# Two-layer recurrent and attention block: one weight prepared from splits throughout, two lower parts built by adding DMAs, and a new order of down products, norm and mixer

## The chip, the cores and the metric

The kernel runs on one core of one Trainium2 chip. The metric is the device time of one execution in microseconds, the median of several runs. The engines are named as the profile names them: PE (TensorE, matrix products; PEld is its weight load), DVE (VectorE), ACT (ScalarE), POOL (GpSimd) and SP (SyncE, which here only issues DMAs). Each engine runs its own instructions in the order that was fixed when the kernel was built, and waits for others through semaphores.

## What is computed

The input x has 4 sequences (the batches b = 0 to 3 below) of 512 rows with 256 columns. There are two layers, and each does `x = x + s * g`, with `xn = layernorm(x)`, a mixer s and a gate g:

```python
# layer 0
s = xn + rmsnorm(y(xn) @ W_out.T, norm_w)   # y is linear in xn: one 256x256 matrix after preparation
g = silu(ffn(xn, W1, W2, W3))
# layer 1
s = attention(layernorm(xn)) + xn           # causal, one head of 256
g = silu(ffn(xn, W1, W2, W3))

def ffn(x, W1, W2, W3):
    hidden = silu(x @ W1.T) * (x @ W3.T)    # 1024 wide
    return fwht(hidden) @ W2.T              # fwht: Hadamard transform of the 1024 columns
```

The recurrence of layer 0 starts from a zero state and is taken for a single step, so it is linear in xn. The Hadamard transform is linear too, so the kernel applies it to W2 once, and never to the hidden values.

## The kernel before

**Splits.** Products must be nearly as exact as fp32. `split` (L59) makes two parts of a tile: `hi`, a copy by ACT rounded to a reduced format (F32R), and `lo = src - hi`, a subtraction by DVE. A product of two split operands is three products: hi·hi, hi·lo and lo·hi (`mm3`, L80; the order is all hi·hi first, then hi·lo and lo·hi in turn for each piece of the contraction). Products of F32R operands are the cheap kind on PE; a product of plain fp32 operands is one instruction in the program and a pair of records in the profile.

**Stages.** Layer 0 is a loop over batches (L997). For each batch `ffn` (L461) goes through 8 chunks of 128 hidden columns: two up products of `mm3` into PSUM banks (`gu`, three banks in turn; chunk 1 of batch 0 borrows two others), SiLU by ACT (L522), the gate multiply by DVE (L523), the split of the result (`hh`, `hl`), and then the down products of an earlier chunk. `defer` says how many chunks wait in the queue before the oldest is taken: all eight in batch 0 (`defer` is NH, since w2 isn't ready), one in batches 1 to 3. In batch 0 the upper parts of the first four chunks go to spare tiles (`early`), and their lower parts are made late, two each in chunks 6 and 7.

**Work beside.** After each half chunk `ffn` calls `slot`, and the object `Beside` (L876) then steps through a list of generators: each task has a number of steps, and slot k of 16 runs steps until the share done is (k + 1)/16 of the total number; the last slot runs all that is left. In batch 0 the tasks are, in this order:

- `prep_first` (L957, 12 steps). It runs `prep_w2` for layer 0: three butterfly steps on DVE for each of two column halves of w2 (scratch tiles come from the pool of the x tiles), then a Hadamard product of 128 on PE. For the first half of layer 0 (`native`, L156) that product takes the fp32 tile and the fp32 matrix `had_f` as they are; for the others the tile is split first and two products with `had` follow (L168). In between come `load_x(1)`, the load of the next batch on SP, and `prep_m` (L187), which builds the mixer's matrix m from win and wout: a scaled split of wout (`wg`), a split of win (`wi`), and 24 products (`mps`).
- `mixer(0)` (L709, 3 steps): products of the transposed xn with m (`o`), squares on ACT, a power on POOL, scaling and adding on DVE. What it adds to xn is used by the gate of batch 0 (`gate_all`), the first task of batch 1.
- `norm(0, 1)` (L426, 3 steps): layer norm of the next batch, its transposes on PE (`xt_1tp`), and their split (`xt`).

In slots of batch 0 the work is queued behind the gate multiply on DVE and behind the last up product on PE (L542).

**w13.** The weights W1 and W3 come in four quarters (q = 0 to 3), each loaded to `w13raw` and split by `split_w13` (L118) when its first chunk (2q) is reached in the program; quarter 0 in two halves.

**Layer 1.** From the end of batch 3 the order on PE is written out by hand (`line["fixed"]`, L66 and L1069): `ffn_s` (L556) has 8 places in each of four rounds q, and the lists in L1085 to L1117 say which steps of attention go there. `pv` (L853) multiplies the softmax by the values and, for each second tile, updates xn by DVE (L871). In round 1, place 7 holds `pv[0]` and `pv[1]`, just after the gate multiply of that round (L668).

Tiles of 4 KB a partition come from one pool of ten (`t4`), which w13raw, w2raw, win, wout and all splits of the preparation share; a tile is taken when an earlier one is free.

Of the kernel before, what the change touches and what calls it, by code (L numbers as in the profile page):

```python
# [11 lines left out]
F32 = mybir.dt.float32  # L12
# [9 lines left out]
P = 128  # L22
# [13 lines left out]
def kernel(ctx: ExitStack, tc: tile.TileContext, a: dict, out: bass.AP):  # L36
# [22 lines left out]
    def split(src, hi, lo, engine=nc.vector):  # L59

        h = nc.scalar.copy(hi, src)  # L61
        return h, engine.tensor_tensor(lo, src, hi.bitcast(F32), ALU.subtract)  # L62

    line = {"fixed": False, "last": None}  # L66
# [10 lines left out]
    def transpose(*args):  # L77
        return in_line(nc.tensor.transpose, *args)

    def mm3(o, terms):  # L80

        seq = [(l[0], r[0]) for l, r in terms]
        for l, r in terms:
            seq += [(l[0], r[1]), (l[1], r[0])]
        for n, (l, r) in enumerate(seq):
            ins = matmul(o, l, r, start=n == 0, stop=n == len(seq) - 1)
        return ins
# [30 lines left out]
    def split_w13(layer, q, raw):  # L118
        both = wp.tile([P, 2, 2, S], F32R, tag="w13", name=f"w13_{layer}_{q}", bufs=4)
        hi, lo = both[:, 0], both[:, 1]  # L120
        if (layer, q) != (0, 0):
            split(raw, hi, lo)
            return hi, lo
        halves = [slice(c * D, (c + 1) * D) for c in range(2)]
        split(*(z[:, :, halves[0]] for z in (raw, hi, lo)))
        next(normed)
        with after(first["norm"][0]), after(first["norm"][1]):
            hi_, lo_ = split(*(z[:, :, halves[1]] for z in (raw, hi, lo)))
        first["w13"] = hi_, lo_
        return hi, lo  # L130
# [8 lines left out]
    def prep_w2(layer, raws, dst, scratch):  # L139

        w2h, w2l = dst
        for half in range(2):
            ds_ = slice(half * P, (half + 1) * P)
            cur = raws[half]
            for st, h in enumerate((1, 2, 4)):
                nxt = scratch(f"w2b{st}_{layer}_{half}", [P, NH, P])
                cv = cur.rearrange("p (g two h) d -> p g two (h d)", two=2, h=h)
                nv = nxt.rearrange("p (g two h) d -> p g two (h d)", two=2, h=h)  # L150
                nc.vector.tensor_tensor(nv[:, :, 0], cv[:, :, 0], cv[:, :, 1], ALU.add)
                nc.vector.tensor_tensor(nv[:, :, 1], cv[:, :, 0], cv[:, :, 1], ALU.subtract)
                cur = nxt
                yield

            native = layer == 0 and half == 0  # L156
            if not native:
                bh = t4(f"w2bh_{layer}_{half}", [P, NH, P], F32R)
                bl = t4(f"w2bl_{layer}_{half}", [P, NH, P], F32R)
                split(cur, bh, bl)  # L160
                yield
            for q in range(2):
                o = psum(f"w2ps_{layer}_{half}_{q}", [P, NH // 2, P])
                qs = slice(q * NH // 2, (q + 1) * NH // 2)
                if native:
                    matmul(o, had_f, cur[:, qs, :], start=True, stop=True)
                else:
                    matmul(o, had, bh[:, qs, :], start=True, stop=False)  # L168
                    matmul(o, had, bl[:, qs, :], start=False, stop=True)
                split(o, w2h[:, qs, ds_], w2l[:, qs, ds_])  # L170
                yield

# [11 lines left out]
        nc.sync.dma_start(win, a["w_in"].rearrange("(c p) i -> p c i", p=P))  # L184
        return win, wout

    def prep_m(win, wout):  # L187

        cb = wp.tile([P, 4, 2, DS], F32, name="cb")
        nc.vector.tensor_tensor(cb, bc[:, :, 0:2, :], bc[:, :, 2:4, :], ALU.mult)  # L190
        cbd = wp.tile([P, 4, DS], F32, name="cbd")
        nc.vector.tensor_tensor(cbd, cb[:, :, 0, :], cb[:, :, 1, :], ALU.subtract)
        g = wp.tile([P, 4], F32, name="g")
        nc.vector.tensor_reduce(g, cbd, AX.X, ALU.add)
        wg = [t4(f"wg{i}", [P, 4, D], F32R) for i in "hl"]
        wi = [t4(f"wi{i}", [P, 4, D], F32R) for i in "hl"]
        for c in range(4):
            nc.scalar.mul(wg[0][:, c, :], wout[:, c, :], g[:, c : c + 1])
            nc.vector.scalar_tensor_tensor(
                wg[1][:, c, :], wout[:, c, :], g[:, c : c + 1], wg[0][:, c, :].bitcast(F32),  # L200
                ALU.mult, ALU.subtract,
            )
        split(win, *wi)
        yield
        hi, lo = (wp.tile([P, 2, D], F32R, name=f"m{i}") for i in "hl")
        o = psum("mps", [P, 2, D])
        for i in range(2):
            mm3(
                o[:, i, :],
                [(tuple(z[:, k, sl(i)] for z in wi), tuple(z[:, k, :] for z in wg)) for k in range(4)],  # L210
            )
        split(o, hi, lo)
        first["m"] = hi, lo
        yield
# [246 lines left out]
    def ffn(name, xT, w13, w2, slot, defer=1, spare=(), parts=1, behind=False, tail=()):  # L461
# [34 lines left out]
        for c in range(NH):  # L496
# [8 lines left out]
            for half in range(parts if c == 0 else 1):  # L505
                n = S // (parts if c == 0 else 1)
                ts_ = slice(half * n, (half + 1) * n)
                if parts == 1 or c:
                    for o, cols in gu:
                        last_up = mm3(o[:, ts_], k_pairs((wh, wl), cols, xT, ts_))  # L510
                    continue

                for n, (w, x) in enumerate(((wh, xT[0]), (wl, xT[0]), (wh, xT[1]))):
                    for o, cols in gu:
                        for k in range(2):
                            last_up = matmul(
                                o[:, ts_], w[:, k, cols], x[:, k, ts_],
                                start=n + k == 0, stop=n + k == 3,
                            )
# [189 lines left out]
    def mixer(b):  # L709

        xn, xT, m = xns[0, b], xTs[0, b], first["m"]
        osb = t4(f"osb{b}", [P, NT, D])
        r = small(f"ssr{b}")
        junk = t2(f"junk{b}", [P, D])
        for i in range(2):
            o = psum(f"o0_{b}_{i}", [P, 2, D])
            for j in range(2):
                mm3(o[:, j, :], k_pairs(xT, sl(2 * i + j), m, ALLD))
            nc.scalar.copy(osb[:, 2 * i : 2 * i + 2, :], o)
            for t in (2 * i, 2 * i + 1):  # L720
                nc.scalar.activation(junk, osb[:, t, :], AF.Square, accum_out=r[:, t : t + 1])
            yield
        nc.vector.tensor_scalar(r, r, 1.0 / D, RMS_EPS, ALU.mult, ALU.add)
        nc.gpsimd.tensor_tensor(r, r, mhalf, ALU.pow)
        for t in range(NT):
            nc.vector.scalar_tensor_tensor(
                osb[:, t, :], osb[:, t, :], r[:, t : t + 1], nwb, ALU.mult, ALU.mult
            )
        nc.vector.tensor_tensor(xn, xn, osb, ALU.add)
        yield  # L730

    class Attention:
# [45 lines left out]
        def tq(self, j):  # L778
            b = self.b
            if j == 0:  # L780
                self.tqs = t4(f"tqh{b}", [P, 2, S], F32R), t4(f"tql{b}", [P, 2, S], F32R)
            o = psum(f"tq{b}_{j}", [P, S])
            mm3(o, k_pairs(first["wqk"], sl(j), self.xg, ALLS))
            split(o, self.tqs[0][:, j, :], self.tqs[1][:, j, :])

        def v(self, i, j):
# [66 lines left out]
        def pv(self, i):  # L853
# [13 lines left out]
                ],  # L867
            )
            if i % 2:
                for t in (i - 1, i):  # L870
                    nc.vector.scalar_tensor_tensor(  # L871
                        xn[:, t, :], self.o[:, t % 2, :], self.rden[:, t : t + 1], xn[:, t, :],
                        ALU.mult, ALU.add,
                    )

    class Beside:  # L876

# [79 lines left out]
    def prep_first():  # L957
# [1 line left out]
        with after(first["w13"][1]):  # L959
            next(steps)  # L960
        yield
        for _ in range(4):
            next(steps)
            yield
        with after(first["silu"]):
            nc.scalar.copy(had, had_f)
        for _ in range(2):
            next(steps)
            yield
        for _ in range(2):  # L970
            next(steps)
            yield
        load_x(1)
        product = prep_m(*raw_m)
        next(product)
        yield
        next(steps)
# [19 lines left out]
    for b in range(B):  # L997
        tasks = []
        if b == 0:
            prep = prep_first()  # L1000
            next(prep)
            tasks.append((prep, 12))
        if b:
            tasks.append((call(gate_all, f"g0_{b - 1}", dn, xns[0, b - 1], xs[b - 1]), 1))
        tasks.append((mixer(b), MIXER))
        if b + 1 < B:
            if b:
                load_x(b + 1)
            if b == 2:
                tasks.append((prep_s(0), 4))  # L1010
            tasks.append((norm(0, b + 1), NORM))
        if b == 0:
            early = w2_tile("early0"), w2_tile("early1")
            spare = [
# [18 lines left out]
        if b == 0:  # L1033
            dn = ffn("f0_0", xTs[0, 0], w13, w2, bg.slot, NH, spare, parts=2, behind=True)
        else:
            tail = [run(atts[0].tq, j) for j in range(2)] if b + 1 == B else []
            dn = ffn(f"f0_{b}", xTs[0, b], w13, w2, bg.slot, tail=tail)
        bg.finish()


# [146 lines left out]
```

## Time and profile before

| | |
|---|---|
| median of 3 runs | 360.51 us (360.42 to 360.60) |
| the profiled execution | 360.78 us |
| its span in the profile | 359.0 us, 6278 instructions |
| DMA | 52.25 MB, mean 146 GB/s |

The profiler records one execution. Its span runs from the first to the last recorded instruction; the 1.8 us between span and time lie around it. In rows of the timeline the columns are the start in us, the time in us, the engine, the line of the source, the operation, the tiles written and read, the shape, and in brackets the idle time before it and what ended it. "f_0gu" is the up product of batch 0, "f_0dn" its down product; in layer 1 the same prefix is used with a round and a letter behind it ("f_0gu2z": batch 0, round 2, bank z). Many lines of the source are helpers (L70 is every matrix product, L61 and L62 are every split), so rows are told apart by their tiles.

The first 36 us, in four stretches of 9 us. The columns are the stretch, its length, busy time and number of instructions of PE, PEld, DVE, ACT and POOL, the granted clock of PE, the DMA share and the rate:

```profile
0.00:9.00 9.00, 7.55 (x28) 6.14 (x29) 5.44 (x17) 3.26 (x6) 1.80 (x7) 1.00 0.70 236
9.00:18.00 9.00, 9.00 (x50) 7.68 (x49) 8.00 (x13) 6.39 (x11) 0.00 (x0) 1.00 0.95 339
18.00:27.00 9.00, 9.00 (x36) 6.59 (x36) 9.00 (x17) 5.77 (x11) 0.00 (x0) 1.00 0.31 93
27.00:36.00 9.00, 9.00 (x51) 7.77 (x50) 9.00 (x17) 5.80 (x11) 0.00 (x0) 1.00 0.58 202
```

PE's ends are modelled, so a 9.00 there says only that no large gap was seen. The starts of successive products tell more.

### The profile page before, as it was taken

To read this page: it belongs to the slowest core of one execution; us is meant where nothing else is said; L and a number is where in the kernel's file an instruction comes from. 1 tells how busy PE (TensorE), PEld (TensorE's weight loads), DVE (VectorE), ACT (ScalarE), POOL (GpSimd) and SP (SyncE) were. 2 spreads that over 40 slices of the span, in tenths; PEclk is the share of its full clock that TensorE was granted. 3 is DMA by queue.
4 is the path that set the end of the run, shared out by engine and by line. 5 is a ranking of instruction groups with operands and counts; after the bars stand their busy time and mean duration, and the time that the engine had idled before them with its cause. 6 is when DMAs were issued, how large, how long until landed. Compare 5 with 4: busy or idle time off the path is not lost.

```text
span 359.0 us, 6278 instructions
## 1 busy us (share of the span) xinstructions
PE 352.4 (98%) x2477; PEld 328.1 (91%) x2477; DVE 287.5 (80%) x597; ACT 197.8 (55%) x373; POOL 20.8 (6%) x22
## 2 busy tenths in 40 slices
PE   8999999999999999999999999999999999999995
PEld 6878998888988898888999999999999999999995
DVE  6899648998579938998886957989669997567645
ACT  3766156266463425674467655576555676556443
POOL 2000110300020210100110001100011000000000
PEclk9999999999999999999999999999999999999999
DMA  7925000301044316656256045572554655445501
GB/s 235 341 91 206 2 1 2 99 18 60 0 157 165 150 39 233 248 180 195 105 207 263 16 190 206 203 224 103 204 179 165 207 186 204 136 151 192 197 2 58
DMA packets 16285, 52.25 MB, mean 146 GB/s; under 512 B 1633, under 2 KB 7937, under 8 KB 16257
## 3 DMA queue, kind: packets, MB, share of 16 engines
q1 hardware_dynamic: 15968, 51.60, 40.9%
q8 instruction: 19, 0.31, 0.4%
q10 hardware_dynamic: 288, 0.26, 0.2%
q14 instruction: 10, 0.07, 0.1%
HBM read 42.40 MB, written 9.45 MB: 144 GB/s over the span
## 4 chain that ended last, share of the span: by engine, by line
PE 96%; DVE 2%; ACT 1%; issue 0%; DVEq 0%
PE f_1dn L70 6%; PE f_2dn L70 6%; PE f_1gu L70 6%; PE f_0gu L70 6%; PE f_2gu L70 6%; PE f_3gu L70 6%; PE f_3dn L70 6%; PE f_0dn L70 6%; PE sc L70 4%; PE pv L70 4%; PE o L70 3%; PE v L70 3%; PE tq L70 3%; PE warm L70 2%; PE w2ps L70 1%; PE pt L70 1%
## 5 line engine op out<-in xcount | busy, mean ns | idle before, releaser
L70 PE MATMUL f_1gu<-xt,w 128*128 128x512 f32 x96 | 24.9, 397 | 0.3 <-ACT xt L61 0.3
L70 PE MATMUL f_3gu<-xt,w 128*128 128x512 f32 x96 | 25.0, 396 | 0.0
L70 PE MATMUL f_2gu<-xt,w 128*128 128x512 f32 x96 | 24.8, 395 | 0.0
L70 PE MATMUL f_0gu<-xt,w 128*128 128x512 f32 (+1 forms) x108 | 24.3, 378 | 0.0
L70 PEld LDWEIGHTS f_0gu<-xt,w 128*128 128x128 f32 x108 | 18.4, 188 | 4.4 <-issue 1.0
L70 PEld LDWEIGHTS f_1gu<-xt,w 128*128 128x128 f32 x96 | 17.0, 188 | 3.6 <-ACT xt L61 0.5
L70 PEld LDWEIGHTS f_2gu<-xt,w 128*128 128x128 f32 x96 | 17.0, 188 | 3.0
L70 PEld LDWEIGHTS f_3gu<-xt,w 128*128 128x128 f32 x96 | 17.0, 188 | 2.9
L61 ACT CAST f_2hh<-f_2h 128x512 fp32r<-128x512 f32 x16 | 9.9, 622 | 15.4 <-DVE f_2h L523 12.3
L70 PE MATMUL f_3dn<-w2l,f_3hh 128*128 128x256 f32 x64 | 17.7, 281 | 0.0
L70 PE MATMUL f_3dn<-w2h,f_3hh 128*128 128x256 f32 x64 | 17.7, 281 | 0.0
L70 PE MATMUL f_1dn<-w2l,f_1hh 128*128 128x256 f32 x64 | 17.7, 282 | 0.0
L70 PE MATMUL f_2dn<-w2h,f_2hh 128*128 128x256 f32 x64 | 17.7, 282 | 0.0
L70 PE MATMUL f_1dn<-w2h,f_1hh 128*128 128x256 f32 x64 | 17.7, 281 | 0.0
L70 PE MATMUL f_2dn<-w2l,f_2hh 128*128 128x256 f32 x64 | 17.6, 281 | 0.0
L70 PE MATMUL f_3dn<-w2h,f_3hl 128*128 128x256 f32 x64 | 17.0, 282 | 0.0
L70 PE MATMUL f_1dn<-w2h,f_1hl 128*128 128x256 f32 x64 | 17.0, 281 | 0.0
L70 PE MATMUL f_2dn<-w2h,f_2hl 128*128 128x256 f32 x64 | 16.7, 281 | 0.0
L61 ACT CAST f_3hh<-f_3h 128x512 fp32r<-128x512 f32 (+1 forms) x17 | 10.0, 594 | 10.2 <-DVE f_3h L523 6.1
L61 ACT CAST f_1hh<-f_1h 128x512 fp32r<-128x512 f32 x16 | 9.9, 622 | 9.7 <-DVE f_1h L523 6.6
L62 DVE TENSOR_TENSOR f_2hl<-f_2h,f_2hh 128x512 fp32r<-128x512 f32 x16 | 10.9, 682 | 3.9 <-ACT f_2hh L61 3.8
L70 PE MATMUL f_0dn<-w2l,f_0hh 128*128 128x256 f32 x48 | 13.7, 286 | 0.0
(487 smaller groups left out, 1147.6 us busy)
## 6 DMA issues: line engine op xcount, KB each, us to landing
sw<-s SPq DMA_DIRECT2D x32, 896.0 KB, 6.4
s<-sp SPq DMA_DIRECT2D x8, 512.0 KB, 3.8
s<-sp SPq DMA_DIRECT2D x8, 384.0 KB, 2.8
w2raw<-in_w SPq DMA_DIRECT2D x4, 512.0 KB, 5.6
sraw<-in_w SPq DMA_DIRECT2D x4, 512.0 KB, 4.3
mrb<-there SPq DMA_DIRECT2D x4, 512.0 KB, 3.7
w13raw<-in_w SPq DMA_DIRECT2D x3, 512.0 KB, 7.1
x<-in_x SPq DMA_DIRECT2D x3, 512.0 KB, 3.6
```

What stands on the lines that cost most here:

```text
L61: h = nc.scalar.copy(hi, src)
L62: return h, engine.tensor_tensor(lo, src, hi.bitcast(F32), ALU.subtract)
L70: ins = call(*args, **kwargs)
```

## The change

1. **w2 of layer 0.** `native` goes: both halves are split and multiplied by `had`. `prep_first` has 13 steps instead of 12, and the cast of `had` comes one step earlier.
2. **Two lower parts by DMA.** A new helper, `split_by_dma`: ACT writes the negated source to `lo`, then the rounded copy to `hi`, and a DMA issued by POOL adds the source to `lo`. It is used for quarter 3 of w13, and for win, whose split moves from `prep_m` into `prep_first`, before the second half of w2.
3. **Order in a sum of three products.** `mm3` takes `late`, which says whose lower part is used last: with 1 the right operand's (the default 0: the left's).
4. **Tasks of batch 0.** `norm(0, 1)` comes ahead of `mixer(0)`, and its steps aren't counted in the total, which is 16 instead of 18.
5. **Down products.** `defer` is 2 instead of 1 in batches 1 to 3.
6. **Attention.** The update of xn in `pv` is queued on DVE behind the last gate multiply (`first["gate"]`).

```diff
+    def split_by_dma(src, hi, lo):
+        nc.scalar.mul(lo, src, -1.0)
+        nc.scalar.copy(hi, src)
+        nc.gpsimd.dma_start(lo.bitcast(F32), src, accum_op=ALU.add)
...
-    def mm3(o, terms):
+    def mm3(o, terms, late=0):
         seq = [(l[0], r[0]) for l, r in terms]
-        for l, r in terms:
-            seq += [(l[0], r[1]), (l[1], r[0])]
+        for side in (1 - late, late):
+            seq += [(l[1 - side], r[side]) for l, r in terms]
...
-        if (layer, q) != (0, 0):
-            split(raw, hi, lo)
+        if q:
+            (split_by_dma if q == 3 else split)(raw, hi, lo)
             return hi, lo
...
-            native = layer == 0 and half == 0
-            if not native:
-                bh = t4(f"w2bh_{layer}_{half}", [P, NH, P], F32R)
-                bl = t4(f"w2bl_{layer}_{half}", [P, NH, P], F32R)
-                split(cur, bh, bl)
-                yield
+            bh, bl = (t4(f"w2b{i}_{layer}_{half}", [P, NH, P], F32R) for i in "hl")
+            split(cur, bh, bl)
+            yield
...
-                if native:
-                    matmul(o, had_f, cur[:, qs, :], start=True, stop=True)
-                else:
-                    matmul(o, had, bh[:, qs, :], start=True, stop=False)
-                    matmul(o, had, bl[:, qs, :], start=False, stop=True)
+                matmul(o, had, bh[:, qs, :], start=True, stop=False)
+                matmul(o, had, bl[:, qs, :], start=False, stop=True)
...
-    def prep_m(win, wout):
+    def prep_m(wi, wout):
...
-        wi = [t4(f"wi{i}", [P, 4, D], F32R) for i in "hl"]
...
-        split(win, *wi)
...
-                        last_up = mm3(o[:, ts_], k_pairs((wh, wl), cols, xT, ts_))
+                        last_up = mm3(o[:, ts_], k_pairs((wh, wl), cols, xT, ts_), late=int(not behind))
...
-                mm3(o[:, j, :], k_pairs(xT, sl(2 * i + j), m, ALLD))
+                mm3(o[:, j, :], k_pairs(xT, sl(2 * i + j), m, ALLD), late=1)
...
-            mm3(o, k_pairs(first["wqk"], sl(j), self.xg, ALLS))
+            mm3(o, k_pairs(first["wqk"], sl(j), self.xg, ALLS), late=1)
...
-                for t in (i - 1, i):
-                    nc.vector.scalar_tensor_tensor(
+                with after(first["gate"]):
+                    for t in (i - 1, i):
+                        nc.vector.scalar_tensor_tensor(
...
-        for _ in range(4):
+        for _ in range(3):
             next(steps)
             yield
         with after(first["silu"]):
@@
-        for _ in range(2):
+        win, wout = raw_m
+        wi = [t4(f"wi{i}", [P, 4, D], F32R) for i in "hl"]
+        split_by_dma(win, *wi)
+        for _ in range(4):
             next(steps)
             yield
         load_x(1)
-        product = prep_m(*raw_m)
+        product = prep_m(wi, wout)
...
-            tasks.append((prep, 12))
+            tasks.append((prep, 13))
...
-        tasks.append((mixer(b), MIXER))
+        if b:
+            tasks.append((mixer(b), MIXER))
...
-            tasks.append((norm(0, b + 1), NORM))
+            tasks.append((norm(0, b + 1), NORM if b else 0))
+        if b == 0:
+            tasks.append((mixer(b), MIXER))
...
-            dn = ffn(f"f0_{b}", xTs[0, b], w13, w2, bg.slot, tail=tail)
+            dn = ffn(f"f0_{b}", xTs[0, b], w13, w2, bg.slot, 2, tail=tail)
```

More of the change, by code (lines that the diff above doesn't have):

```diff
@@ L869, in pv @@
             if i % 2:
-                for t in (i - 1, i):
[L871 to L874, printed above, removed]
+                with after(first["gate"]):
+                    for t in (i - 1, i):
+                        nc.vector.scalar_tensor_tensor(
+                            xn[:, t, :], self.o[:, t % 2, :], self.rden[:, t : t + 1], xn[:, t, :],
+                            ALU.mult, ALU.add,
+                        )
     class Beside:
```

## The prediction

> **What bounds the kernel now.** I read the shares of busy time first, then the chain that ended last.
>
> ```profile
> PE 352.4 (98%) x2477; PEld 328.1 (91%) x2477; DVE 287.5 (80%) x597; ACT 197.8 (55%) x373; POOL 20.8 (6%) x22
> PE 96%; DVE 2%; ACT 1%; issue 0%; DVEq 0%
> ```
>
> PE is 96% of the chain: from its first real product at 8.16 us to the last gate at 354.9 us nearly every microsecond is a product. So I price every edit by one question: does PE do less, or wait less? VectorE or ScalarE time that is saved or added counts only where it makes PE wait. The granted clock is 1.00 in every stretch I asked for, so products cost the same everywhere: starts of successive 128x512 products are 0.233 us apart (6 in 1.40 us in the chain), of 128x256 products 0.118 us.
>
> To find PE's waits I went along the starts of its products, looking for a distance above these. Leaving the start-up, four places stand out. Two are work of an expensive kind, in the chain in order of time:
>
> ```profile
> 18.22 0.86 PE w2ps L70 x2
> 19.07 1.40 PE f_0gu L70 x6
> 20.48 0.86 PE w2ps L70 x2
> ```
>
> Each pair of records is one product of the plain fp32 Hadamard matrix with half of w2's first column half (L166), 0.86 us; the same shape from split operands costs 0.233 us a product. The other two are true waits. Layer 0, from batch 0 to batch 1 (timeline of PE):
>
> ```profile
> 51.18 0.28 PE L70 MATMUL f_0dn<-w2h,f_0hl 128*128 128x256 f32 x1
> 51.79 0.73 PE L70 MATMUL f_1gu<-xt,w 128*128 128x512 f32 x2 [0.33 <-ACT xt L61]
> ```
>
> The starts lie 0.61 us apart where 0.12 would do: 0.49 us, waiting for ScalarE's cast of batch 1's transposed input. And layer 1, batch 0 (timeline of all engines):
>
> ```profile
> 193.61 0.87 DVE L871 SCALAR_TENSOR_TENSOR xn<-pv,rden,xn 128x256 f32<-128x256 f32 x2
> ...
> 194.03 0.60 PE L70 MATMUL xt_1tp<-ident,xn 128*128 128x128 f32 x4
> ...
> 194.40 0.68 DVE L668 TENSOR_TENSOR f_0h<-f_0h,f_0gu1l 128x512 f32<-128x512 f32 x1
> ...
> 195.22 0.94 PE L70 MATMUL f_0gu2z<-tb,sw 128*128 128x256 f32 x6 [0.59 <-DVE f_0h L668]
> ```
>
> The four transposes would be through at 194.03 + 4 x 0.11 = 194.47; the next product starts at 195.22: 0.75 us lost. It needs the PSUM bank that L668 reads, and VectorE did two residual updates (L871) first.
>
> **Part by part.** *w2 from splits.* Removed: two native products, 2 x 0.86 = 1.72 us of PE. Added: four split products, 4 x 0.233 = 0.93. **-0.78 us**, with nothing beside it to hide it. Also added: one ScalarE cast (row w2bh, 1.05 us) and one VectorE subtraction (row w2bl, 1.21 us). They make half 0's w2 later, but its first use is by a down product at 32.49, and the last butterfly of that half ended at 16.73 + 0.68 = 17.41; plus 2.3 us is 19.7. Covered.
>
> *Norm ahead of the mixer.* Batch 1's normalised input was complete at 41.78 + 1.38 = 43.2, but its transposes ran at 49.82 to 51.1, behind the mixer and nearly all down products. Put ahead of the mixer, they need only run one microsecond earlier: **-0.49 us**. What is late next is VectorE's lower half of xt (52.48, two by 1.28 us together), which moves with them. If they don't move, 0; more than 0.49 can't be had. The mixer goes last instead; its result is needed only by the gate of batch 0, in batch 1's first slot, and nothing on PE stands there behind it.
>
> *Residual updates behind the gate multiply.* L668's own input (SiLU) is ready at 192.88 + 0.59 = 193.47, so it can take the update's place at 193.61, end at 194.29, and PE follow 0.14 later as it did (195.08 to 195.22): 194.43, before the transposes end. **-0.75 us**. The updates move back 0.6 us, to end at 195.1; the PSUM bank they free is of a pool whose next use is the transposes at 196.72. In batches 1 and 2 L668 starts at 240.92 and 287.50, right when its own SiLU allows, behind the update already: nothing to gain.
>
> *Two lower parts by DMA.* VectorE loses the third big split of w13 (25.41) and that of win (30.59) and gains w2bl: 1.22 + 1.21 - 1.21 = -1.22 us. ScalarE gains two negated copies and a cast, 3 x 1.05 = 3.15 us, in a stage where it is busy 18.0 of 27 us. No engine's sum binds PE here; dates do.
>
> ```profile
> 15.97 1.06 ACT L61 CAST w<-w13raw 128x1024 fp32r<-128x1024 f32 x1
> 16.92 0.63 ACT L531 CAST early<-f_0h 128x512 fp32r<-128x512 f32 x1
> 17.44 0.61 ACT L522 ACTIVATE f_0h<-f_0gu 128x512 f32<-128x512 f32 x1
> ...
> 25.41 1.22 DVE L62 TENSOR_TENSOR w<-w13raw,w 128x1024 fp32r<-128x1024 f32 x1
> ```
>
> The w13 copy can be done at 15.97 + 1.05 = 17.0 and the DMA go. No DMA of this kind is in the trace. From below, the nearest row, also 512 KB leaving SBUF (the stores of prepared splits, "s<-sp ... 512.0 KB, 3.8" us to landing); from above, the same size in the crowded start, win, 8.7 us. I take 3.8, since the DMA share falls from 0.95 before 18 us to 0.31 after it. It lands at 20.8 (at worst 25.7), while VectorE delivered that part at 26.6 and PE did not wait. POOL, which issues it, has nothing from 6.7 to 40.7 us, so nobody is queued behind it. win's part is used from 34.13; win itself landed at 9.73 + 8.7 = 18.4, so ten microseconds remain. Price 0.
>
> A rule speaks against it. The Trainium skill (SBUF — State Buffer, "SBUF: two separate sides" and "A bandwidth-pool intuition that's wrong") says a DMA issued from GpSimd starves while VectorE holds the port pair they share: 620 ns become 3100 ns beside a VectorE copy. The trace has no such DMA but shows POOL beside a busy VectorE:
>
> ```profile
> 48.59 1.01 POOL L724 TENSOR_TENSOR ssr<-ssr,mhalf 128x4 f32<-128x4 f32 x1 [6.85 <-DVE ssr L723]
> 104.47 1.91 POOL L724 TENSOR_TENSOR ssr<-ssr,mhalf 128x4 f32<-128x4 f32 x1 [36.90 <-DVE ssr L723]
> ```
>
> The same instruction takes 1.01 us with VectorE idle and 1.91 beside it. By the rule's factor of five the DMA would be 19 us, land at 36 and hold PE up for most of ten microseconds: an estimate of +5 to +8. By the row's factor of 1.9 it takes 7.2 us and lands at 24, free. I go by the row, also because what VectorE does from 16 to 30 us is nearly all TENSOR_TENSOR, which the same page says has no two-port mode.
>
> *Fewer fillers, more ScalarE.* The native products filled PE at 18.05 while the SiLU of 17.44 freed a bank for the next product (18.51). Now PE wants that bank at 18.05, and ScalarE has another 1.05 us to do near it. From 0 (the copy goes elsewhere; ScalarE is idle 1.15 us before 21.37) to 1.05 (the copy goes ahead of the SiLU). I take **+0.3 us**, nearer to 0, because PE had other ready products in this stage and never waited between 8.4 and 51.2.
>
> *The rest.* Down products a chunk later (batches 1 to 3), the order inside a sum of three products, prep steps spread over more slots, load_x(1) two slots later on SP (the row sits at 21.58, its first reader in VectorE at 34.73): same instructions, other places. PE's pauses in batches 1 to 3 are seven of 0.08 us, 0.6 in all, so -0.6 is the most they can give; new ones can come. I take 0.
>
> Sum: -0.78 - 0.49 - 0.75 + 0.30 = **-1.72 us**. The profiled execution took 360.78 (span 359.0 and 1.8 around it), 0.27 above the median of 360.51. Applied to the median: **358.8 us**. Its own range: 357.9 (no ScalarE delay, and half the small pauses gone) to 359.6 (ScalarE's full delay).
>
> **Rivals.** *The freed time is given back in the first stage (359.8 us).* VectorE is busy 26.0 of the 27 us from 9 to 36, and ends its last lower half of batch 0 at 40.6, only 1.7 us ahead of PE's first use of a chunk that is not kept early (42.35). PE, 1.3 us ahead, runs into it. Then only layer 1's 0.75 stays. For it: VectorE's full row. Against: its load falls by 1.2.
>
> *The DMAs are late (slower: 362.8 us).* Place: the last quarter of w13, products of chunks 6 and 7 around 26 us. It decides from a DMA longer than about 9 us (17.0 to 26). Price: landing at 30 costs some 4 us of PE, since PE's order is set when the kernel is built: -1.7 + 4 = +2.3. For it: a DMA that adds has to read what it writes, and the rule above. Against: four to five microseconds of slack at the price I chose.
>
> *Scattered new waits (360.4 us).* A reordered program gets 0.5 us in each of three batches, 1.6 with batch 0. Against: PE has waited little in any order seen here.
>
> *The updates don't move* (the hold falls on an older gate): 359.5 us, inside the likeliest's range.
>
> **Chances.** A measurement here tells apart about 0.2%, 0.72 us: same is 359.8 to 361.2. Forecast 0.56 (all but 0.01 faster); given back 0.20 (0.11 faster, 0.09 same); scattered 0.08 (0.05 same, 0.03 slower); DMAs late 0.16, slower. Faster 0.66, same 0.15, slower 0.19. The range for 8 in 10 goes from 357.8 to 361.5: it leaves out most of the late DMAs and a little below.
>
> **What would show it.** Right: w2ps takes 0.23 us in every row; no gap ahead of f_1gu; L668 of batch 0 ahead of L871 and f_0gu2z right behind the transposes; a POOL DMA of about 4 us and no PE wait on w before 30 us. Wrong: PE waiting for a DMA in chunks 6 and 7 or in the mixer's weight product; PE waiting for f_0h (SiLU) near 18 us; gaps in f_1 to f_3 that were not there.

## The result and the profile after

The changed kernel takes **362.25 us** (361.35 to 362.68, 6 runs) beside 360.54 for the kernel before: 1.0045 times as long, 95% interval 1.0031 to 1.006. The profiled execution took 362.68 us with a span of 360.9, 1.9 more than before. The forecast of 358.8 us was wrong in sign, and the time lies above its range.

The shares of the chain that ended last, of the changed kernel:

```profile
PE 82%; DVE 8%; ACT 3%; DMA 2%; SPq 1%; issue 1%; POOL 0%; DVEq 0%
```

PE was 96% of this chain; now 18% of it is others, VectorE first. (The changed kernel's lines stand elsewhere in the source: L76 is every matrix product, L666 the gate multiply that was L668.) PE's waits, in the view of who waited for whom (total, number, longest, in us; f_1hl is the lower half of a hidden chunk of batch 1, f_1dn the down product that uses it):

```profile
PE f_1dn L76 <- DVE f_1hl L62: 2.1, 2, 1.6
...
PE f_0gu L76 <- ACT f_0h L520: 0.8, 1, 0.8
PE f_2dn L76 <- DVE f_2hl L62: 0.2, 1, 0.2
```

Counted as in the prediction, by the distance of product starts above the usual one, these are 0.63 and 1.78 us in batch 1, 1.00 us near 18 us, and 0.35 us in batch 2. About 0.1 us is lost besides right behind each, in all some 4.2 us. Against them stand the native products (0.78) and the wait ahead of f_1gu (0.49, and 0.10 behind it): 2.8 of the 3.1 us that layer 0 loses. The attention edit pays 1.3 us in layer 1.

To keep the two apart, and free of the start-up, which differs by some tenths from run to run, I measured two stretches in each trace: from PE's first up product (8.16 us before) to its first up product of layer 1, and from there to PE's last product. Before they are 163.47 and 182.82 us. The times in the table are medians, but the stretches are those of the one profiled execution. For the changed kernel it lies 0.43 us above the median, for "quarter 3 split as before" 0.51 above, for "edit 5 undone" 0.58 below and for "edits 1 and 2" 0.59 below; where these differ, the medians decide.

| kernel | us | ratio to before | layer 0 | layer 1 |
|---|---|---|---|---|
| after, all six edits | 362.25 | 1.0045 | +3.13 | -1.34 |
| edit 4 undone | 359.47 | 0.9973 | -0.02 | -1.32 |
| quarter 3 of w13 split as before | 362.86 | 1.0067 | +4.23 | -1.34 |
| edit 5 undone | 363.28 | 1.0076 | +3.48 | -1.33 |
| edit 4 and that quarter undone | 359.55 | 0.9972 | +0.18 | -1.32 |
| edit 4 undone, copies held back | 359.25 | 0.9962 | +0.17 | -1.34 |
| all edits, no end of mixer(0) | 359.87 | 0.9981 | +0.73 | -1.29 |
| edit 4 alone | 364.58 | 1.0112 | +4.57 | -0.33 |
| edit 4 alone, norm counted | 361.62 | 1.0031 | +1.35 | -0.39 |
| edit 6 alone | 359.20 | 0.9963 | +0.01 | -1.22 |
| edit 1 alone | 361.55 | 1.0031 | +1.03 | +0.11 |
| edits 1 and 2 | 360.93 | 1.0009 | -0.16 | +0.09 |
| edits 1, 2 and 6 | 359.68 | 0.9976 | +0.50 | -1.22 |

### The profile page after: what moved, and what is told of

The parts are those of the page before. It is cut to its first block, busy times and chain, and to the rows that moved or that the text cites. A ratio compares the mean times of both kernels' runs of the same rounds, so it can differ in the third digit from the quotient of the medians.

```text
span 360.9 us, 6287 instructions
## 1 busy us (share of the span) xinstructions
PE 352.0 (98%) x2477; PEld 327.6 (91%) x2477; DVE 285.9 (79%) x596; ACT 200.3 (55%) x376; POOL 23.3 (6%) x24
## 3 DMA queue, kind: packets, MB, share of 16 engines
q0 software_dynamic: 288, 1.05, 1.6%
## 4 chain that ended last, share of the span: by engine, by line
PE 82%; DVE 8%; ACT 3%; DMA 2%; SPq 1%; issue 1%; POOL 0%; DVEq 0%
PE f_0dn L76 6%; PE f_3gu L76 6%; PE f_3dn L76 6%; PE f_1dn L76 5%; PE f_2dn L76 5%; PE sc L76 4%; PE pv L76 4%; PE f_0gu L76 4%; PE v L76 3%; PE f_2gu L76 3%; PE tq L76 3%; PE f_1gu L76 2%; DMA w13raw<-in_w 2%; PE o L76 2%; DVE osb L724 1%; PE pt L76 1%
## 5 line engine op out<-in xcount | busy, mean ns | idle before, releaser
L76 PE MATMUL f_3gu<-xt,w 128*128 128x512 f32 x96 | 24.7, 395 | 0.0
L76 PE MATMUL f_0gu<-xt,w 128*128 128x512 f32 (+1 forms) x108 | 23.6, 371 | 0.8 <-ACT f_0h L520 0.8
L76 PE MATMUL f_1gu<-xt,w 128*128 128x512 f32 x96 | 24.4, 395 | 0.0
L76 PE MATMUL f_2gu<-xt,w 128*128 128x512 f32 x96 | 24.3, 395 | 0.0
L76 PEld LDWEIGHTS f_0gu<-xt,w 128*128 128x128 f32 x108 | 18.3, 188 | 4.9 <-ACT f_0h L520 1.5
L76 PEld LDWEIGHTS f_1gu<-xt,w 128*128 128x128 f32 x96 | 17.3, 188 | 3.5
L76 PEld LDWEIGHTS f_2gu<-xt,w 128*128 128x128 f32 x96 | 17.2, 188 | 3.3
L76 PEld LDWEIGHTS f_3gu<-xt,w 128*128 128x128 f32 x96 | 17.1, 188 | 3.2
L76 PE MATMUL f_1dn<-w2h,f_1hl 128*128 128x256 f32 x64 | 17.5, 284 | 2.1 <-DVE f_1hl L62 2.1
L76 PE MATMUL f_3dn<-w2h,f_3hh 128*128 128x256 f32 x64 | 18.0, 282 | 0.0
L76 PE MATMUL f_3dn<-w2l,f_3hh 128*128 128x256 f32 x64 | 17.9, 281 | 0.0
L76 PE MATMUL f_1dn<-w2h,f_1hh 128*128 128x256 f32 x64 | 17.9, 282 | 0.0
L76 PE MATMUL f_1dn<-w2l,f_1hh 128*128 128x256 f32 x64 | 17.9, 282 | 0.0
L76 PE MATMUL f_2dn<-w2h,f_2hh 128*128 128x256 f32 x64 | 17.8, 282 | 0.0
L76 PE MATMUL f_3dn<-w2h,f_3hl 128*128 128x256 f32 x64 | 17.7, 282 | 0.0
L76 PE MATMUL f_2dn<-w2l,f_2hh 128*128 128x256 f32 x64 | 17.7, 281 | 0.0
L76 PE MATMUL f_2dn<-w2h,f_2hl 128*128 128x256 f32 x64 | 16.9, 282 | 0.2 <-DVE f_2hl L62 0.2
L76 PEld LDWEIGHTS f_1dn<-w2h,f_1hl 128*128 128x128 f32 x64 | 11.8, 189 | 3.0 <-DVE f_1hl L62 3.0
```

Of the source, the lines that this page charges most:

```text
L76: ins = call(*args, **kwargs)
```

## Where the loss sits: VectorE idle, then late

VectorE around the end of batch 0, in stretches (length, busy time of PE, PEld, DVE, ACT, POOL, with the number of instructions, then PE's granted clock, the DMA share and the rate). The kernel before:

```profile
43.00:54.00 11.00, 10.67 (x83) 10.16 (x83) 4.66 (x10) 5.29 (x14) 1.01 (x1) 1.00 0.00 1
54.00:75.00 21.00, 21.00 (x125) 18.36 (x123) 20.01 (x43) 9.54 (x22) 3.42 (x2) 1.00 0.17 51
```

The changed kernel:

```profile
43.00:54.00 11.00, 11.00 (x87) 10.60 (x86) 2.13 (x5) 5.32 (x13) 0.00 (x0) 1.00 0.00 0
54.00:75.00 21.00, 18.91 (x108) 15.92 (x107) 20.01 (x41) 8.01 (x20) 6.40 (x3) 1.00 0.12 35
```

From 43 to 54 us VectorE works 2.13 us instead of 4.66, though it has no less to do in all. From 54 to 75 it was full already before (20.01 of 21) and is as full now, so the work that came in pushes other work back, and PE is busy 2.1 us less there. What VectorE did from 48 to 56 us in the kernel before (timeline):

```profile
48.34 0.17 DVE L723 TENSOR_SCALAR ssr<-ssr 128x4 f32<-128x4 f32 x1 [5.18 <-ACT junk L721]
49.63 1.67 DVE L726 SCALAR_TENSOR_TENSOR osb<-osb,ssr,nwb 128x256 f32<-128x256 f32 x4 [1.12 <-POOL ssr L724]
51.34 1.23 DVE L729 TENSOR_TENSOR xn<-xn,osb 128x1024 f32<-128x1024 f32 x1
...
53.68 1.28 DVE L698 TENSOR_TENSOR g_0g<-g_0g,xn 128x512 f32<-128x512 f32 x2
54.88 1.28 DVE L700 TENSOR_TENSOR x<-x,g_0g 128x512 f32<-128x512 f32 x2
```

What arrives late now is seen in the chain of the changed kernel from 54 to 75 us:

```profile
54.80 1.02 POOL ssr L722
55.84 1.68 DVE osb L724 x4
...
59.33 1.14 DVE xn L727
...
63.65 1.08 DVE g_0g L696 x2
...
69.02 0.80 DVE x L698 x2
...
73.84 0.61 DVE f_1hl L62
74.45 0.04 issue
74.50 0.51 PE f_1dn L76 x2
```

The first L724 and L727 are the end of batch 0's mixer, its tail (L726 and L729 before, 49.63 to 52.57); L696 and L698 are the gate of batch 0 that waits for it (L698 and L700 before, 53.68 to 56.2). They now stand in the middle of batch 1, among the butterflies of layer 1's w2 (L158) and batch 2's norm, and ahead of the lower half of a hidden chunk that PE wants at 72.7 us. The delay begins on PE: the mixer's products ran at 39.5 and from 43.65 to 46.0 us before, and at 45.9 to 48.0 and 50.9 to 52.3 after, begun only with the transposes of the norm that now stands ahead of them. Their end is 6.3 us later and the start of the tail 6.2.

## The experiments

Theory A: edit 4 throws the mixer's tail into batch 1. Theory B: deferring the down products makes the waits. Theory C: the negated copy on ScalarE holds PE near 18 us. Theory D came later: what the w2 products save is spent on other waits of the first stage.

**Edit 4 undone** (mixer(0) ahead of norm(0, 1) again, all steps counted):

```diff
-        if b:
-            tasks.append((mixer(b), MIXER))
+        tasks.append((mixer(b), MIXER))
...
-            tasks.append((norm(0, b + 1), NORM if b else 0))
-        if b == 0:
-            tasks.append((mixer(b), MIXER))
+            tasks.append((norm(0, b + 1), NORM))
```

> The changed kernel with edit 4 alone undone (in batch 0 the mixer again ahead of the norm, both counted). Theory A (the mixer, being last in batch 0, throws its tail on VectorE into batch 1, where the lower halves of the hidden chunks then come late): PE's waits for f_1hl (0.6 and 1.8 us) and f_2hl (0.35 us) go, the wait of 0.5 us ahead of f_1gu may come back: 359.5 to 360.3. Theory B (the waits come from down products taken a chunk later): they stay, about 362.2 to 362.7. In both the wait of 1.0 us for a SiLU near 18 us stays.

359.47 us, 0.9973 (0.9962 to 0.9984). All waits for f_1hl and f_2hl are gone: A holds, B falls. The one ahead of f_1gu is gone too, although edit 4 is not there to remove it. Left in PE's waits:

```profile
PE o L76 <- DVE w2l L62: 0.4, 1, 0.4
PE f_0gu L76 <- ACT f_0h L520: 0.4, 1, 0.4
```

By starts, 0.60 and 0.55 us, each with 0.1 behind it: 1.36 us, about what the native products and f_1gu's wait had given (1.37), so -0.02 in layer 0. That the two agree so closely is chance, since the SiLU wait changes from run to run (below).

**Quarter 3 of w13 split as before** (`split` in place of `split_by_dma` there):

> The changed kernel with the last quarter of w13 split as before (cast by ScalarE, subtraction by VectorE), the rest as changed. Theory C (the negated copy on ScalarE ahead of a SiLU holds PE 1.0 us near 18 us): that wait goes or falls under 0.2 us, 361.2. Rival (VectorE's row is so full that the 1.2 us given back to it costs as much, or the cast of w2's first half takes the place of the copy): 362.2, or a wait of the same size elsewhere before 36 us.

362.86 us: on the time the rival is right. The SiLU wait falls to 0.62 us only, since two casts of w13 stand ahead of that SiLU as they did before (it ends at 18.33, before at 18.05) and no native product fills PE meanwhile. But w13's third quarter also landed late in this execution (timeline of ScalarE, the changed kernel):

```profile
13.91 1.05 ACT L61 CAST w<-w13raw 128x1024 fp32r<-128x1024 f32 x1 [1.29 <-DMA w13raw<-in_w]
```

And this one:

```profile
14.11 1.05 ACT L61 CAST w<-w13raw 128x1024 fp32r<-128x1024 f32 x1 [1.85 <-DMA w13raw<-in_w]
...
17.73 0.60 ACT L520 ACTIVATE f_0h<-f_0gu 128x512 f32<-128x512 f32 x1
```

From the start of that cast to the end of the SiLU it takes 5.16 us in the changed kernel and 4.22 here, so the negated copy does cost that SiLU 0.94 us, as C says. Counted from PE's first up product (8.22 and 7.78) the cast starts 0.64 us later here; with the landing of the changed kernel the wait would have been about nothing (an estimate from these figures). Two new waits come, 0.56 us for a gate multiply and 0.47 us ahead of a down product, and the one for f_2hl grows to 0.63. So the DMA seems worth having: all four runs without it are slower than all six with it, by 0.6 us between the medians.

**Edit 5 undone** (`defer` 1 again):

> The changed kernel with down products in batches 1 to 3 again one chunk behind, the rest as changed. Theory A (mixer's tail): the waits for f_1hl stay or grow, since the lower half is wanted one chunk sooner: 362.2 to 363.5. Theory B (deferring is the cause): they go, 359.5.

363.28 us, 1.0 above the changed kernel. The waits for f_1hl are the same 0.6 and 1.8 us, those for f_2hl grow to 0.64 and one for f_3hl (0.69) comes. (Layer 0 is only 0.35 longer in the profiled execution, because its SiLU wait was 0.31 us in place of 1.00.) Deferring is a help where VectorE is late; the loss isn't its work.

**Edit 4 and that quarter undone:**

> The changed kernel with both undone, the task order of batch 0 and the DMA for the last quarter of w13. Theories A and C together: neither the SiLU wait nor the f_1hl waits, 358.6 to 359.3, faster than before. If the first stage gives back what it gains: 360.5.

359.55 us, above what A and C gave. The SiLU wait is gone, but waits of 0.16 and 0.55 us stand around w2's products near 29 us and the 0.60 ahead of the mixer's product stays.

**Edit 4 alone**, on the kernel before:

> The kernel before with edit 4 alone (norm ahead of mixer in batch 0, the norm's steps not counted; total 12 + 3). Theory A (mixer's tail thrown into batch 1): 0.5 us gained ahead of f_1gu, 2.5 to 3.5 us lost to waits for f_1hl, more than in the changed kernel since the down products follow one chunk behind: 362.5 to 363.6. Rival (the loss needs the other edits): 360.0.

364.58 us, beyond the expectation: this edit alone costs 4 us. With down products one chunk behind, PE waits 2.12 us for f_1hl, 0.65 for f_2hl and 0.78 for f_3hl; the wait ahead of f_1gu is gone, but another of 0.49 us, for a gate multiply, stands at an up product later in batch 1, and one of 0.39 us near 31 us.

**Edit 4 alone, norm counted as before** (`NORM` in place of `NORM if b else 0`):

> The kernel before with norm ahead of mixer in batch 0, but the norm's three steps counted as before (total 18, so that norm falls in slots 10 to 12 and the mixer in the last three). If the order of the two is what throws the mixer's tail into batch 1: as slow as edit 4 alone, 363.5 to 365. If it was the last slot that did it (mixer run as a whole at the end): 360.0 to 361.0.

361.62 us, between the two. Mixer's tail on VectorE starts at 52.27 us (before 49.63, edit 4 alone 57.63). So both parts of edit 4 count: the order costs some 1.3 us of layer 0, and that the mixer falls as a whole into the last slot the other 3.2. Of the waits that the order brings, only 0.23 us is for f_1hl; 0.65 is for f_2hl and 0.62 for f_3hl, in batches 2 and 3. Why VectorE comes late there was not found.

**All edits, without the end of mixer(0)** (its power on POOL, scaling and adding left out in batch 0, so the output of that batch lacks the mixer in layer 0):

> The changed kernel, leaving out for batch 0 the end of the mixer: the power on POOL, the scaling by VectorE and the adding to xn (2.9 us of VectorE), so the output of layer 0's first batch lacks the mixer. Theory A: the waits for f_1hl go or shrink by most of their 2.4 us, 359.9 to 360.6. Rival (it is not the tail's load but the order of PE or the gate's own work in batch 1): waits stay above 1.5 us, 361.5 or more.

359.87 us, no wait for f_1hl. Without 2.9 us of tail, the gate, which need not wait for it any more, runs at 50.1 to 52.7 us in what was VectorE's gap. That supports A by another road: with less on VectorE, f_1hl is in time, though the mixer's products on PE are as late as in the changed kernel. It doesn't tell the tail from the gate, since both have left the full stretch. f_2hl (0.41) and the SiLU wait (1.11) stay, so the wait for f_2hl isn't the tail's work alone.

**Edit 6 alone:**

> The kernel before with edit 6 alone (residual updates in attention queued behind the gate multiply). If the wait of 0.75 us ahead of f_0gu2z is all of it: 359.8, that wait gone and the rest of the trace as before. If something else takes its place: 360.5.

359.20 us, more than the 0.75 us expected: layer 1 is 1.22 us shorter. The stretches up to the third round of each batch show 0.82 us in batch 0, and about 0.18 each in batches 1 and 2.

**Edit 4 undone, and the copies for w13 held back** (`with after(...)` the SiLU of chunk 3 around `split_by_dma` for q = 3):

> The changed kernel with edit 4 undone, and the two ScalarE copies for the last quarter of w13 queued behind the SiLU of chunk 3. Theory C (the negated copy ahead of a SiLU is what holds PE near 18 us): the 0.55 us wait for f_0h seen there goes, 358.9. Rival (PE's front simply runs into VectorE and ScalarE in this stage): a wait of the same size appears a few microseconds later, 359.5. If the DMA now lands too late for chunk 6, PE waits for w instead: 360 or more.

359.25 us. The SiLU wait is gone and the DMA, issued at 20.5, is in time, but 0.24 us and some tenths appear from 25 to 29 us, and 0.42 for f_2hl. So the time lies between the two, a little nearer to the rival, and layer 0 has gained nothing (+0.17). The wait for f_2hl is there although the tail is in its old place.

**Edit 1 alone:**

> The kernel before with edit 1 alone (both halves of layer 0's w2 from splits; 13 steps). Theory D (the 0.78 us of PE is taken in the first stage only if VectorE, which gains 1.2 us of work here, is not ahead of PE's need): PE's native products go but waits on VectorE of at least 0.5 us appear before 45 us, 360.2 to 361.0. Rival (PE's saving counts in full, as the prediction had it): 359.75.

361.55 us, slower than both said. The native products are gone (0.78) and layer 0 is still 1.03 us longer: waits of 0.18, 0.55 and 0.41 us with the tenths behind them stand at w2's and the mixer's products from 28 to 31.7 us; the profile names a gate multiply for the second and ScalarE's cast of win for the third.

**Edits 1 and 2:**

> The kernel before with edits 1 and 2 (w2 from splits, two lower parts by DMA). Theory D: VectorE has 1.2 us less than before in the first stage, so less is lost to it, but ScalarE's copies stand ahead of a SiLU near 18 us (0.5 to 1.0 us): 360.0 to 360.7. Rival (savings count in full): 359.75.

360.93 us, just above the range given. Its -0.16 in layer 0 is too good, since the profiled execution was the fastest of twelve. Between the medians, taking two subtractions from VectorE returns 0.6 us of the 1.0 that edit 1 lost. The wait ahead of f_1gu, still 0.49 us with edit 1 alone, is gone here, with the mixer ahead of the norm as before.

**Edits 1, 2 and 6:**

> The kernel before with edits 1, 2 and 6, thus without the order of sums, the task order and the deferred down products. Theory D: as edit 6 alone (359.2) within 0.5 us, since edits 1 and 2 together bring about nothing. Rival (savings count in full): 358.4.

359.68 us, 0.48 above edit 6 alone, within what D said. Its SiLU wait is 0.99 us here and 0.32 in edits 1 and 2, with the same order of ScalarE there. How long that wait is follows when w13's third quarter lands: its cast starts 5.75 us after PE's first up product here and 5.08 there.

## Why the prediction failed, step by step

**The failed step is "Norm ahead of the mixer".** It said of the mixer that "its result is needed only by the gate of batch 0, in batch 1's first slot, and nothing on PE stands there behind it". I looked for who waits for the result, and not for what is queued behind the instructions that make it. Behind them, on VectorE's own queue, stand the lower halves of batch 1's chunks, and PE does wait for those. The step cost 3.15 us of layer 0 (+3.13 with it, -0.02 without), 2.8 by the medians, where -0.49 was priced. Nor was it needed for that gain: with edits 1 and 2 alone the wait ahead of f_1gu is gone, though the mixer still comes first. The profile of the kernel before had the warning: VectorE was nearly free from 43.2 to 49.6 us and then did the tail, whereas its stretch from 54 to 75 was already 20.01 of 21 us full. Moving 2.5 us of its work (4.66 to 2.13) from the first into the second could not be free.

**w2 from splits: right about PE, wrong about the sum.** The products shrank as worked out, but edits 1, 2, 3 and 5 together bring nothing: -0.02 in layer 0, and with edit 6 beside them 359.47 us where edit 6 alone has 359.20. This is the rival "given back in the first stage", which had 0.20: the waits that take the gain end with work of VectorE and ScalarE. "Covered" looked at the down product that uses w2, and not at the other work of these two engines that the added cast and subtraction push back.

**The SiLU near 18 us: right mechanism, wrong size.** +0.3 was taken out of 0 to 1.05; it was 1.00 us in the profiled execution of the changed kernel, with the copy and the cast both ahead of the SiLU (timeline of ScalarE, changed kernel):

```profile
16.06 1.06 ACT L66 ACTIVATE w<-w13raw 128x1024 fp32r<-128x1024 f32 x1
17.02 1.04 ACT L67 CAST w<-w13raw 128x1024 fp32r<-128x1024 f32 x1
17.96 0.61 ACT L529 CAST early<-f_0h 128x512 fp32r<-128x512 f32 x1
18.48 0.59 ACT L520 ACTIVATE f_0h<-f_0gu 128x512 f32<-128x512 f32 x1
```

The six executions that have both ahead of it waited 0.31, 0.32, 0.55, 0.99, 1.00 and 1.11 us, on the whole the longer the later w13's third quarter landed (its cast starts 5.08 us after PE's first up product in the two shortest, 5.69 to 5.87 in the three longest). So no single figure was right, and this alone moves layer 0 by up to 0.8 us between executions. "PE had other ready products" was the wrong reason: those that had filled PE at 18.05 were the native products, which the same change took away.

**The DMAs: right.** Issues of the changed kernel (bytes, us to landing):

```profile
w<-w13raw POOLq DMA_DIRECT2D x1, 512.0 KB, 4.8
wil<-win POOLq DMA_DIRECT2D x1, 512.0 KB, 4.7
```

3.8 was taken and 7.2 came from the row of POOL. In the other runs such DMAs took 4.6 to 6.5 us, the longest where both were under way at once. The 19 came from two figures of the Trainium skill (SBUF — State Buffer, "A bandwidth-pool intuition that's wrong (but worth ruling out)"), about 620 ns alone and about 3100 ns beside a VectorE copy. Taken as a factor of five they were misread: the same section says that such a DMA is not slowed in proportion but waits until VectorE lets the port go. Beside a VectorE that worked 7.9 of the 9 us from 18 to 27, all of it TENSOR_TENSOR, no starving of that size is seen, and no product waited for a DMA. So it is chance that the measured time comes close to the 362.8 us of the rival "The DMAs are late".

**Residual updates: right, and under-priced.** L666 now comes first, and the next product follows without a wait (timeline, changed kernel):

```profile
196.79 0.68 DVE L666 TENSOR_TENSOR f_0h<-f_0h,f_0gu1l 128x512 f32<-128x512 f32 x1
...
197.39 0.87 DVE L870 SCALAR_TENSOR_TENSOR xn<-pv,rden,xn 128x256 f32<-128x256 f32 x2
...
197.57 0.97 PE L76 MATMUL f_0gu2z<-tb,sw 128*128 128x256 f32 x6
```

-1.22 measured for -0.75. "Nothing to gain" in batches 1 and 2 missed some 0.18 us in each, of which waits of 0.11 and 0.13 us before that same product were in the trace, below what I looked for.

**The rest at 0**: deferring the down products gave 1.0 us between the medians beside edit 4, where VectorE is late; without edit 4 its worth is not known.

**Signs and range.** Two of the signs named for being wrong came: PE waiting for f_0h near 18 us, and gaps in f_1 and f_2 that were not there. The lower end of the range, 357.9, has a slip: without ScalarE's delay and with half of the small pauses gone the sum gives 358.2, and 357.9 only with all of them gone. It doesn't bear on the miss.

The best kernel seen needs one edit out of six: edit 6 alone, 359.20 us, 0.9963 (0.9948 to 0.9977). Edit 4 undone with the copies held back is the same within the error.

What stays open: a kernel in which the first stage keeps what w2's products save wasn't found; what makes f_2hl late where the tail isn't moved is not known; why edit 4 alone shortens layer 1 by 0.33 us was not followed; and edits 2, 3 and 5 weren't tried by themselves.

## What to carry to other kernels

When work is moved to a later time, ask what stands behind it on its own engine in the place where it lands; the reader of its result is only half the question, and an idle stretch before a full one is the warning. When PE is the bound and never waits in a stage, its cheaper products pay only as far as the engines that feed it have slack there. Of the three edits that were tried by themselves (1, 4 and 6), the one whose sign held swaps neighbours in one engine's queue at a wait that was seen. And where a wait depends on when a load lands, one traced execution is no measure of it.

## What was not expected of the hardware

POOL's power of 128x4 elements took 1.01 us beside an idle VectorE and 1.91 at most before; in the changed kernel one took 3.72 us while VectorE ran TENSOR_TENSOR rows without a gap (timeline of POOL):

```profile
71.59 3.72 POOL L274 TENSOR_TENSOR ln_2r<-ln_2r,mhalf 128x4 f32<-128x4 f32 x1 [8.99 <-DVE ln_2r L273]
```

A DMA that adds to what is already in SBUF took 4.7 to 4.8 us for 512 KB in the changed kernel, and kept POOL itself for 0.86 to 1.05 us.
